# Zeroing the embedding rows of item 0: by products on TensorE, or by a multiplication on ScalarE

## The chip, the cores and the metric

One core of a Trainium2 chip runs the whole kernel. The metric is the device time of one launch in microseconds. Three runs of the kernel before took 1643.39 us in the median (1637.56 to 1649.35).

## What is computed

The inputs are 1024 sequences of 50 item numbers, their lengths, an embedding table of 100,001 rows of 128 numbers, and two vectors gamma and beta. Row 0 of the table counts as zero. Cut to what matters:

```python
emb = emb_table.at[0].set(0.0)
e = emb[seq]                                   # 1024 x 50 x 128
prefix = jnp.cumsum(e, axis=1)
denom = jnp.minimum(t_idx[None, :], lengths[:, None])
uF = prefix / denom[:, :, None]
mean = uF.mean(axis=0); var = uF.var(axis=0)
y = (uF - mean) * lax.rsqrt(var + BN_EPS) * gamma + beta
# for each of 50 time steps, x = y[:, t]:
v = v + (x - v) / 2.0
spike = (v - 1.0 >= 0)
v = v - spike
# and at the end:
scores = spikes.mean(axis=0) @ emb.T           # 1024 x 100001
```

So there is a recurrent part of 50 steps, whose result is a count of spikes per sequence and feature, and a large product with the whole table, whose output is 409.6 MB.

## The kernel before, in words

**Recurrent stage.** The 1024 sequences lie as 8 blocks (n) of 128. For each time step t the function `gather` (line 204) issues eight indirect DMAs from GpSimd (POOL), each fetching 128 table rows into one block of the tile `e`; `e` has two buffers, so the gather of step t+2 writes where step t lay. TensorE transposes each block with the identity and adds it up in PSUM (line 327): the accumulators `pre[0]` and `pre[1]` hold the running sums with features on the partitions and 512 sequences each. This document calls the eight transposes of a step T0 to T7. VectorE divides (`uF`, line 338) and takes the statistics (lines 339 and 345). ScalarE takes the root (349) and subtracts the mean (356); VectorE works out the factor `a` in a few short instructions (362 to 375); ScalarE forms x in the PSUM tile of v (379); VectorE adds the spikes of the step before to `count` (300) and finishes v (382); ScalarE copies v less 1 into `d` (293), from which VectorE forms `negv` in the next step (297).

**Item 0.** The gather fetches the real row 0 where an item is 0, and the running sums have to lose it. `zT` holds, for each step and sequence, whether the item is 0 (lines 215 to 226). `correct(t, l)` (line 279) adds, for each half of the sequences, one product of `ls` with `zT`, which subtracts row 0 where it was gathered. `only(t)` (line 266) makes the left sides `ls` for five steps at a time on VectorE. The first such product also opens the accumulation group of `pre` (start=True). `correct(t + 1, l)` is issued after the eight transposes of step t.

**The order.** The tile framework runs with a manual schedule: each engine takes its instructions in the order in which the program issues them and waits by semaphores for what it needs from other engines. What stands behind a waiting instruction on its engine waits too.

**The end of the stage.** In the last step T4, T5 and T6 are each followed by four transposes that only keep TensorE busy (`keep_busy`, line 307), and T7 by sixteen more (line 414). At steps 42 and 44 the kernel also prepares the first two blocks of the table (`prepare`, line 148: eight transposes, a copy on ScalarE, a subtraction on VectorE), and after the second it fetches two more table blocks from SP (line 404). The last step is cut into pieces, so that the first output block can start when the first 128 sequences have their counts.

**Product stage.** The table comes in blocks of 1024 rows, is transposed (line 136) and split into a high and a low part (152, 153), and is multiplied with the counts of 128 sequences at a time (160). ScalarE and VectorE take turns in moving the results out of PSUM (513 and 511), and SP stores them.

**Buffers.** The pool `once` holds what lasts for the recurrent stage; after the stage its place is taken by output tiles. Its tiles `near`, `centred` and `vA` of the last step lie in the places of `r0`, `r0hi` and `r0n`.

Of the kernel before, what the change touches and what calls it, by code (L numbers as in the profile page):

```python
# [12 lines left out]
F32 = mybir.dt.float32  # L13
BF16 = mybir.dt.bfloat16
F32R = mybir.dt.float32r
I32 = mybir.dt.int32
U32 = mybir.dt.uint32
AF = mybir.ActivationFunctionType
ALU = mybir.AluOpType

P = 128
# [4 lines left out]
BANK = 512  # L26
GROUP = 6
AHEAD = 6
ONLY = 5
TWICE = 2  # L30
ASIDE = 2
SHIFT = TWICE + ASIDE
# [7 lines left out]
def rec_kernel(  # L40
# [9 lines left out]
    nc = tc.nc  # L50
    B, T = seq.shape
    N, D = table.shape
# [119 lines left out]
    with ExitStack() as ph:  # L172
# [9 lines left out]
        nc.sync.dma_start(out=idx, in_=seq.rearrange("(p n) t -> p n t", n=NB))  # L182
        len_i = once.tile([P, NB], I32, tag="len_i", name="len_i")
        nc.sync.dma_start(out=len_i, in_=lengths.rearrange("(p n) -> p n", n=NB))
        r0 = once.tile([P, D], F32, tag="r0", name="r0")
        nc.sync.dma_start(out=r0, in_=table[0:1, :].to_broadcast([P, D]))
        gb = once.tile([P, 2], F32, tag="gb", name="gb")
        nc.sync.dma_start(out=gb[:, 0:1], in_=gamma.rearrange("(d o) -> d o", o=1))
        nc.sync.dma_start(out=gb[:, 1:2], in_=beta.rearrange("(d o) -> d o", o=1))
# [22 lines left out]
                )  # L212

        make_identity(nc, ident)
        isz = up.tile([P, NB, P], F32, tag="uF", name="isz")
        rb = up.tile([P, NB, P], F32, tag="uF", name="rb")
        gather(0)

        nc.vector.memset(isz, 0.0)
        for u in (0, P // 2):  # L220
            nc.vector.tensor_single_scalar(isz[:, :, u : u + T], idx, 0.0, ALU.is_equal)
        zps = vp.tile([P, B], F32, tag="v1", name="zps")
        for n in range(NB):
            nc.tensor.transpose(zps[:, n * P : (n + 1) * P], isz[:, n, :], ident)
        zT = once.tile([P, B], F32R, tag="zT", name="zT")
        nc.scalar.copy(zT, zps)
        r0hi = once.tile([P, D], F32R, tag="r0hi", name="r0hi")
        nc.scalar.copy(r0hi, r0)
        r0n = once.tile([P, D], F32, tag="r0n", name="r0n")
        nc.vector.tensor_scalar_mul(r0n, r0hi.bitcast(F32), -1.0)  # L230
        up2 = slice(P // 2, P)
        nc.vector.tensor_tensor(r0n[up2, :], r0hi[up2, :].bitcast(F32), r0[up2, :], ALU.subtract)
        sel = once.tile([P, P // 2], F32, tag="sel", name="sel")
        nc.vector.tensor_tensor(sel, ident[:, : P // 2], ident[:, P // 2 :], ALU.add)


        rl = once.tile([P, NB], F32, tag="rl", name="rl")
        nc.vector.tensor_copy(rl, len_i)
# [22 lines left out]

        pre = [accp.tile([P, BANK], F32, tag=f"pre{h}", name=f"pre{h}") for h in range(B // BANK)]

        ls = once.tile([P, ONLY, D], F32R, tag="ls", name="ls")

        def only(t):

            k = t % ONLY
            if k == 0:
                n = min(ONLY, T - t)  # L270
                nc.vector.tensor_tensor(
                    ls[:, :n, :],
                    r0n.unsqueeze(1).to_broadcast([P, n, D]),
                    sel[:, t : t + n].unsqueeze(2).to_broadcast([P, n, D]),
                    ALU.mult,
                )
            return ls[:, k, :]

        def correct(t, l):
            for h in range(B // BANK):  # L280
                nc.tensor.matmul(  # L281
                    pre[h],
                    lhsT=l,
                    rhs=zT[:, h * BANK : (h + 1) * BANK],
                    start=t == 0,
                    stop=False,
                    skip_group_check=True,
                )

        def over(t, v):  # L290

            d = lp.tile([P, B], BF16, tag="d", name=f"d_{t}")
            nc.scalar.activation(d, v, AF.Identity, bias=less)  # L293
            return d
# [4 lines left out]
        def spiked(out, cs, v):  # L299
            nc.vector.scalar_tensor_tensor(out, v, V_TH, count[:, cs], ALU.is_ge, ALU.add)  # L300
# [9 lines left out]

        v = None

        correct(0, only(0))
        l = only(1)
        gather(1)
        for t in range(T):
            last = t == T - 1
            e = es.pop(t)
            if last:
                rest(d, v, pieceA)  # L320
                near = once.tile([P, P], F32, tag="r0", name="near")
                nc.vector.tensor_scalar(near, negv[:, :P], -0.5, hgb[:, 1:2], ALU.mult, ALU.add)
            uF = up.tile([P, B], F32, tag="uF", name=f"uF_{t}")
            bs = sp.tile([P, B // BANK, 6], F32, tag="bs", name=f"bs_{t}")
            for h, cs in enumerate(halves):
                for k in range(0, BANK, P):
                    nc.tensor.matmul(  # L327
                        pre[h][:, k : k + P],
                        lhsT=e[:, h * BANK + k : h * BANK + k + P],
                        rhs=ident,  # L330
                        start=False,
                        stop=last,
                        is_transpose=True,
                        skip_group_check=True,
                    )
                    if last and h and k + P < BANK:
                        keep_busy(ident, KQ // 2)
                nc.vector.scalar_tensor_tensor(uF[:, cs], rlen[:, cs], 1.0 / (t + 1), pre[h], ALU.max, ALU.mult)  # L338
                nc.vector.bn_stats(bs[:, h, :], uF[:, cs])  # L339
            if t + 2 < T:  # L340
                gather(t + 2)
            if not last:
                correct(t + 1, l)
            mv = sp.tile([P, 2], F32, tag="mv", name=f"mv_{t}")
            nc.vector.bn_aggr(mv, bs.rearrange("p h s -> p (h s)"))  # L345


            r = sp.tile([P, 1], F32, tag="r", name=f"r_{t}")
            nc.scalar.activation(r, mv[:, 1:2], AF.Sqrt, bias=eps)  # L349
            if last:  # L350
                centred = once.tile([P, P], F32, tag="r0hi", name="centred")
                nc.vector.tensor_scalar(centred, uF[:, :P], mv[:, 0:1], hgb[:, 2:3], ALU.subtract, ALU.mult)
                w = sp.tile([P, 1], F32, tag="w", name="w")
                nc.vector.tensor_scalar_add(w, mv[:, 1:2], BN_EPS)
            else:
                nc.scalar.activation(uF, uF, AF.Identity, bias=mv[:, 0:1], scale=-1.0)


            if t and not last:
                rest(d, v, whole)  # L360

            nc.vector.reciprocal(r, r)
            q = sp.tile([P, 1], F32, tag="q", name=f"q_{t}")
            a = sp.tile([P, 1], F32, tag="a", name=f"a_{t}")
            if last:
                nc.vector.tensor_scalar(q, w, r, r, ALU.mult, ALU.mult)
                nc.vector.scalar_tensor_tensor(q, q, 3.0, r, ALU.subtract, ALU.mult)
                vA = once.tile([P, P], F32, tag="r0n", name="vA")
                nc.vector.scalar_tensor_tensor(vA, centred, q, near, ALU.mult, ALU.add)
                spiked(countA, slice(0, P), vA)  # L370
                nc.vector.tensor_mul(a, q, hgb[:, 0:1])
            else:
                nc.vector.scalar_tensor_tensor(q, mv[:, 1:2], BN_EPS, r, ALU.add, ALU.mult)
                nc.vector.tensor_scalar(q, q, r, 3.0, ALU.mult, ALU.subtract)
                nc.vector.tensor_scalar(a, q, r, hgb[:, 0:1], ALU.mult, ALU.mult)  # L375


            def x(vt, cs):
                nc.scalar.activation(vt, uF[:, cs], AF.Identity, bias=hgb[:, 1:2], scale=a)  # L379

            def step(vt, cs):
                nc.vector.scalar_tensor_tensor(vt, negv[:, cs], -0.5, vt, ALU.mult, ALU.add)  # L382

            if not last:
                vt = vp.tile([P, B], F32, tag=f"v{t % 2}", name=f"v_{t}")
                x(vt, whole)
                if t:
                    spiked(count, whole, v)
                step(vt, whole)
                v = vt  # L390
                if t == T - 2:
                    spiked(count, whole, v)
                d = over(t, v)
                if t + 2 < T:
                    l = only(t + 2)

                if t in (T - 8, T - 6):
                    q = (t - T + 8) // 2
                    pair(q)
                    prepare(q, vp.tile([P, HALF], F32, tag="v1", name=f"pt_{q}"))  # L400
                    if q == TWICE - 1:
                        for k in range(TWICE):
                            rows[GROUP + ASIDE + k] = first[:, k, :]
                        nc.sync.dma_start(
                            out=first[:, :TWICE, :],
                            in_=table[(GROUP + ASIDE) * HALF : (GROUP + SHIFT) * HALF, :].rearrange(
                                "(q p k) d -> p q (k d)", p=P, k=KQ
                            ),
                        )

        keep_busy(near, 2 * KQ)
# [138 lines left out]
```

## Time and profile before

| | |
|---|---|
| median of three runs | 1643.39 us |
| the profiled execution | 1576.4 us |
| its span in the trace | 1574.6 us |
| first and last gather on POOL start | 3.6 and 504.5 us |
| POOL busy | 380.9 us in 406 instructions |
| ScalarE (ACT) busy | 673.4 us |
| VectorE (DVE) busy | 949.3 us |
| TensorE (PE) busy | 1128.4 us |
| written to memory | 409.60 MB |

In the profile, a line such as "L207" is a line of the kernel below. A row of the groups gives the line, the engine, the operation, the tiles written and read, the count, then the busy time in microseconds and the mean of one in nanoseconds, then the idle time ahead of these instructions and what ended it. "PEld" is the load of the stationary operand. "issue" is time in which an engine waited for nothing that the profile shows. A line of the timeline gives the start and the duration in microseconds, and in brackets the idle time before it with what ended it. The chain of waits is followed back from the last instruction, at each step to what released it.

### The profile page before, as it was taken

What the parts mean: (1) busy time and instruction counts of PE and PEld (TensorE: products, weight loads), DVE (VectorE), ACT (ScalarE), POOL (GpSimd) and SP (SyncE); (2) the same over time, 40 slices, a digit from 0 to 9 for tenths busy, and PEclk for the clock granted to TensorE, in tenths of its full rate; (3) what the DMA queues carried; (4) which work ended last, traced back from release to release, by engine and by line L of the source; (5) the groups of instructions that cost most, each with busy time, mean ns of one, the idle gap of its engine ahead of it and who ended that gap; (6) DMA issues with size and microseconds to landing.
All of it is one profiled execution on the core that took longest, in us unless ns stands there. A gap on an engine that the chain in (4) does not pass through costs nothing.

```text
span 1574.6 us, 12255 instructions
## 1 busy us (share of the span) xinstructions
PE 1128.4 (72%) x4464; PEld 799.5 (51%) x4464; DVE 949.3 (60%) x1127; ACT 673.4 (43%) x697; POOL 380.9 (24%) x406
## 2 busy tenths in 40 slices
PE   4544444444445998899888878888878878888884
PEld 2211111111122766677766666666666666666663
DVE  5777777777777655666555555555555545555552
ACT  2333333333333545555444444444444444444442
POOL 7777777777776000000000000000000000000000
PEclk9999999999975999999999999898999999999998
DMA  9711111111121899999999999999999999999998
GB/s 347 264 52 54 52 54 52 53 53 54 52 79 47 337 414 414 423 413 402 428 427 429 427 426 421 421 409 429 421 428 424 402 428 429 414 423 417 426 405 354
DMA packets 51313, 488.12 MB, mean 310 GB/s; under 512 B 10079, under 2 KB 10336, under 8 KB 30004
## 3 DMA queue, kind: packets, MB, share of 16 engines
q1 hardware_dynamic: 30752, 430.86, 65.1%
q0 software_dynamic: 12800, 26.24, 5.7%
q10 hardware_dynamic: 7700, 30.23, 4.7%
q8 instruction: 35, 0.57, 0.1%
q14 instruction: 26, 0.21, 0.0%
HBM read 77.69 MB, written 409.60 MB: 309 GB/s over the span
## 4 chain that ended last, share of the span: by engine, by line
DMA 48%; POOL 18%; PE 15%; issue 8%; DVE 5%; ACT 4%; ACTq 0%; SPq 0%; POOLq 0%; DVEq 0%
DMA scores<-o 42%; POOL e L207 18%; PE po L160 14%; DMA e<-in_L_rec_emb_table,idx 6%; DVE o L511 3%; ACT o L513 3%; DVE pairs L153 1%; ACT pairs L152 0%; PE pt L136 0%; ACT hi L152 0%; DVE lo L153 0%; PE pre L327 0%; DMA idx<-in_r_seq 0%; DVE bs L339 0%; DVE uF L338 0%
## 5 line engine op out<-in xcount | busy, mean ns | idle before, releaser
L511 DVE TENSOR_SCALAR o<-po 128x1024 f32<-128x1024 f32 (+1 forms) x391 | 467.3, 1214 | 329.5 <-DMA scores<-o 187.4
L513 ACT ACTIVATE o<-po 128x1024 f32<-128x1024 f32 x391 | 392.0, 1025 | 506.0 <-DMA scores<-o 362.7
L207 POOL DMA_INDIRECT e<-in_L_rec_emb_table,idx x400 | 380.2, 951 | 123.9 <-issue 112.5
L327 PE MATMUL pre<-ident,e 128*128 128x128 f32 x400 | 179.9, 463 | 227.3 <-DMA e<-in_L_rec_emb_table,idx 227.0
L160 PE MATMUL po<-pairs,countB 128*128 128x512 f32 (+1 forms) x1120 | 292.8, 408 | 57.8 <-ACT o L513 57.8
L160 PE MATMUL po<-pairs,countC 128*128 128x512 f32 (+1 forms) x840 | 240.1, 433 | 59.4 <-ACT o L513 53.4
L160 PEld LDWEIGHTS po<-pairs,countB 128*128 128x128 f32 x1120 | 211.8, 194 | 119.2 <-ACT o L513 76.7
L327 PEld LDWEIGHTS pre<-ident,e 128*128 128x128 f32 x400 | 73.4, 184 | 337.1 <-DMA e<-in_L_rec_emb_table,idx 336.4
L160 PEld LDWEIGHTS po<-pairs,countC 128*128 128x128 f32 x840 | 168.1, 208 | 112.1 <-ACT o L513 65.5
L153 DVE TENSOR_TENSOR pairs<-pt,pairs 128x1024 fp32r<-128x1024 f32 x70 | 85.2, 1218 | 94.9 <-ACT pairs L152 94.8
L338 DVE SCALAR_TENSOR_TENSOR uF<-rlen,pre 128x512 f32<-128x512 f32 x100 | 68.3, 683 | 109.6 <-PE pre L327 109.6
L136 PE MATMUL pt<-ident,rows 128*128 128x128 f32 (+1 forms) x768 | 104.4, 281 | 9.9 <-issue 4.9
L349 ACT ACTIVATE r<-mv,eps 128x1 f32<-128x1 f32 x50 | 14.7, 295 | 223.4 <-DVE mv L345 223.4
L136 PEld LDWEIGHTS pt<-ident,rows 128*128 128x128 f32 (+1 forms) x768 | 94.1, 147 | 27.1 <-issue 10.9
L160 PE MATMUL po<-hi,countB 128*128 128x512 f32 x208 | 85.6, 411 | 15.1 <-ACT o L513 13.5
L281 PE MATMUL pre<-zT,ls 128*128 128x512 f32 x100 | 77.5, 777 | 23.2 <-DVE uF L338 19.3
L152 ACT CAST pairs<-pt 128x1024 fp32r<-128x1024 f32 x70 | 70.1, 1014 | 41.2 <-PE pt L136 41.2
L160 PE MATMUL po<-lo,countB 128*128 128x512 f32 x208 | 83.4, 401 | 0.0
L293 ACT ACTIVATE d<-v,less 128x1024 bf16<-128x1024 f32 x49 | 54.6, 1114 | 64.8 <-DVE v L382 62.3
L160 PE MATMUL po<-hi,countC 128*128 128x512 f32 x156 | 66.7, 427 | 14.1 <-ACT o L513 12.6
L379 ACT ACTIVATE v<-uF,hgb,a 128x1024 f32<-128x1024 f32 x49 | 59.2, 1208 | 30.6 <-DVE a L375 30.5
L339 DVE BATCH_NORM_STATS2 bs<-uF 128x6 f32<-128x512 f32 x100 | 69.4, 694 | 3.5
(87 smaller groups left out, 851.8 us busy)
## 6 DMA issues: line engine op xcount, KB each, us to landing
scores<-o SPq DMA_DIRECT2D x96, 3072.0 KB, 19.8
scores<-o SPq DMA_DIRECT2D x32, 1536.0 KB, 8.9
scores<-o SPq DMA_DIRECT2D x30, 1024.0 KB, 7.9
rows<-in_L_rec_emb_table ACTq DMA_DIRECT2D x19, 1536.0 KB, 29.3
scores<-o SPq DMA_DIRECT2D x8, 2896.5 KB, 17.2
rows<-in_L_rec_emb_table SPq DMA_DIRECT2D x5, 3072.0 KB, 34.9
e<-in_L_rec_emb_table,idx POOLq DMA_INDIRECT x400, 2.5
rows<-in_L_rec_emb_table SPq DMA_DIRECT2D x2, 1024.0 KB
```

What stands on the lines that cost most here:

```text
L136: nc.tensor.transpose(pt[:, k0 : k0 + pw], r[:pw, k0 : k0 + D], ident[:pw, :pw])
L152: nc.scalar.copy(vh, vp)
L153: nc.vector.tensor_tensor(vl, vp, vh.bitcast(F32), ALU.subtract)
L160: nc.tensor.matmul(po[:, :kw], lhsT=counts[n], rhs=part[:, k0 : k0 + kw], start=j == 0, stop=j == 1,)
L207: nc.gpsimd.indirect_dma_start(out=es[t][:, n * P : (n + 1) * P], out_offset=None, in_=table, in_offset=bass.IndirectOffsetOnAxis(ap=idx[: ...
L281: nc.tensor.matmul(pre[h], lhsT=l, rhs=zT[:, h * BANK : (h + 1) * BANK], start=t == 0, stop=False, skip_group_check=True,)
L327: nc.tensor.matmul(pre[h][:, k : k + P], lhsT=e[:, h * BANK + k : h * BANK + k + P], rhs=ident, start=False, stop=last, is_transpose=True, ...
L338: nc.vector.scalar_tensor_tensor(uF[:, cs], rlen[:, cs], 1.0 / (t + 1), pre[h], ALU.max, ALU.mult)
L339: nc.vector.bn_stats(bs[:, h, :], uF[:, cs])
L379: nc.scalar.activation(vt, uF[:, cs], AF.Identity, bias=hgb[:, 1:2], scale=a)
L511: nc.vector.tensor_scalar_mul(o[:, h0 : h0 + hw], po[:, :hw], 1.0 / T)
L513: nc.scalar.mul(o[:, h0 : h0 + hw], po[:, :hw], 1.0 / T)
```

## The change

Where an item is 0, the gathered row is now multiplied by 0, and by 1 elsewhere. `some` holds these factors. For each block of each step ScalarE runs one in-place multiplication of 128 by 128 elements with one factor per partition (sequence), `masked`. For step t+1 these are issued within step t: blocks 0 to 3 between x (379) and the copy `d` (293), blocks 4 to 7 after `d` (and, at steps 42 and 44, after the copy of the table block). The eight of step 0 come before the loop. The products `correct`, their left sides `only`, and the tiles for them are gone. The accumulation groups are opened by one product per half with `count`, which is zero at that time.

```diff
-        r0 = once.tile([P, D], F32, tag="r0", name="r0")
-        nc.sync.dma_start(out=r0, in_=table[0:1, :].to_broadcast([P, D]))
...
-        nc.vector.memset(isz, 0.0)
-        for u in (0, P // 2):
-            nc.vector.tensor_single_scalar(isz[:, :, u : u + T], idx, 0.0, ALU.is_equal)
...
+        some = once.tile([P, NB, T], F32, tag="some", name="some")
+        nc.vector.tensor_single_scalar(some, idx, 0.0, ALU.is_gt)
...
-        def only(t):
...
-        def correct(t, l):
...
+        def masked(t, ns):
+
+            for n in ns:
+                part = es[t][:, n * P : (n + 1) * P]
+                nc.scalar.activation(part, part, AF.Identity, scale=some[:, n, t : t + 1])
...
-        correct(0, only(0))
-        l = only(1)
+        for h in range(B // BANK):
+            nc.tensor.matmul(
+                pre[h],
+                lhsT=count[:, :P],
+                rhs=count[:, h * BANK : (h + 1) * BANK],
+                start=True,
+                stop=False,
+                skip_group_check=True,
+            )
+        masked(0, range(NB))
         gather(1)
...
             if t + 2 < T:
                 gather(t + 2)
-            if not last:
-                correct(t + 1, l)
...
                 if t == T - 2:
                     spiked(count, whole, v)
+                masked(t + 1, range(NB // 2))
                 d = over(t, v)
-                if t + 2 < T:
-                    l = only(t + 2)
-
                 if t in (T - 8, T - 6):
...
+                masked(t + 1, range(NB // 2, NB))
```

More of the change, by code (lines that the diff above doesn't have):

```diff
@@ L28 @@
 AHEAD = 6
-ONLY = 5
 TWICE = 2
@@ L214, in rec_kernel @@
         make_identity(nc, ident)
-        isz = up.tile([P, NB, P], F32, tag="uF", name="isz")
         rb = up.tile([P, NB, P], F32, tag="uF", name="rb")
         gather(0)
-        nc.vector.memset(isz, 0.0)
-        for u in (0, P // 2):
-            nc.vector.tensor_single_scalar(isz[:, :, u : u + T], idx, 0.0, ALU.is_equal)
[L222 to L234, printed above, removed]
+        some = once.tile([P, NB, T], F32, tag="some", name="some")
+        nc.vector.tensor_single_scalar(some, idx, 0.0, ALU.is_gt)
         rl = once.tile([P, NB], F32, tag="rl", name="rl")
@@ L262, in rec_kernel @@
         pre = [accp.tile([P, BANK], F32, tag=f"pre{h}", name=f"pre{h}") for h in range(B // BANK)]
-        ls = once.tile([P, ONLY, D], F32R, tag="ls", name="ls")
-        def only(t):
[L268 to L277, printed above, removed]
-        def correct(t, l):
[L280 to L288, printed above, removed]
+        def masked(t, ns):
+            for n in ns:
+                part = es[t][:, n * P : (n + 1) * P]
+                nc.scalar.activation(part, part, AF.Identity, scale=some[:, n, t : t + 1])
         def over(t, v):
```

## The prediction

> **What bounds the kernel now.** I read the table of stretches first, then the chain of waits over two parts, then the groups, then one step of the loop in the timeline.
>
> ```profile
> 300.00:400.00 100.00, 47.54 (x100) 19.00 (x100) 71.91 (x123) 36.62 (x41) 75.62 (x81) 1.00 0.18 53
> 1000.00:1574.00 574.00, 460.11 (x1992) 361.12 (x1990) 297.36 (x252) 248.05 (x250) 0.00 (x0) 0.92 0.98 416
> ```
>
> Busy us of PE, PEld, DVE, ACT and POOL, then clock, DMA share and GB/s. There are two stages. Up to about 510 us the cell runs 50 time steps: POOL is busiest (75.6 of 100), the DMA engines carry 18%. After it the product writes 409.6 MB with the DMA engines at 98%. The change touches the first stage only, so it counts by how much later the first product starts. The chain of waits over 150 to 260 us, and two groups:
>
> ```profile
> by line: POOL e L207 57.7%; issue 23.2%; DMA e<-in_L_rec_emb_table,idx 19.5%; PE pre L327 0.4%; POOLq L207 0.1%
> ...
> L207 POOL DMA_INDIRECT e<-in_L_rec_emb_table,idx x400 | 380.2, 951 | 123.9 <-issue 112.5 <-DMA e<-in_L_rec_emb_table,idx 7.3 <-DMA idx<-in_r_seq 2.3
> L281 PE MATMUL pre<-zT,ls 128*128 128x512 f32 x100 | 77.5, 777 | 23.2 <-DVE uF L338 19.3 <-DVE ls L271 3.9
> ```
>
> POOL issues a gather of 128 rows every 0.95 + 0.30 = 1.25 us: 8 a step, 10.0 us a step, 500 us for 50. The gathers run from 3.6 to 505.4 us. The products that go (L281) are not in the chain at all. One step of the timeline shows how much room the other engines have:
>
> ```profile
> 315.45 0.94 POOL L207 DMA_INDIRECT e<-in_L_rec_emb_table,idx  x1 [0.30 <-issue]
> ...
> 316.75 0.48 PE L327 MATMUL pre<-ident,e 128*128 128x128 f32 x1 [0.77 <-DMA e<-in_L_rec_emb_table,idx]
> ...
> 318.96 0.30 ACT L349 ACTIVATE r<-mv,eps 128x1 f32<-128x1 f32 x1 [4.41 <-DVE mv L345]
> 319.16 1.13 ACT L356 ACTIVATE uF<-uF,mv 128x1024 f32<-128x1024 f32 x1
> ...
> 320.56 0.27 DVE L375 TENSOR_SCALAR a<-q,r,hgb 128x1 f32<-128x1 f32 x1
> ...
> 320.93 1.21 ACT L379 ACTIVATE v<-uF,hgb,a 128x1024 f32<-128x1024 f32 x1 [0.64 <-DVE a L375]
> 322.18 1.23 DVE L382 SCALAR_TENSOR_TENSOR v<-negv,v 128x1024 f32<-128x1024 f32 x1 [0.21 <-ACT v L379]
> 323.44 1.11 ACT L293 ACTIVATE d<-v,less 128x1024 bf16<-128x1024 f32 x1 [1.30 <-DVE v L382]
> ```
>
> Count from S = 316.75, the start of the eighth transpose T7, when its block lands. x ends at S+5.4, v is ready at S+6.66, d runs S+6.7 to S+7.8. Then ScalarE waits 4.4 us for the next step. The buffer that T7 frees is written again by a gather about 8.2 us later (307.23 to 315.45, one step earlier): POOL does not wait until the compute is 8 us late.
>
> **What the skill says.** The Trainium skill, ScalarE: Activation LUTs, What ACT_TABLE_LOAD costs: 186 ns + 0.833 ns per element, about 93 ns more for each operand that is a [128,1] pointer, and 93 ns of overlap between neighbours. The trace agrees: L349 (one pointer) takes 295 ns, yet L356 starts 0.20 us after it, and the one small copy (L228, 128x128) took 0.30 against 0.29 by the formula. SBUF — State Buffer, SBUF: two separate sides: only VectorE and GpSimd share a port, ScalarE has its own. So the masks should not stretch the gathers; before, POOL holds its 1.25 us beside ScalarE's work.
>
> **The change, part by part.**
>
> *Removed.* Setup (isz, zps, zT, r0hi, r0n, sel: DVE 0.9 + 0.65 + 0.75, ACT 1.3), 10 ls products of 0.81 us, 100 products of 0.78 us. All lie beside POOL's issue, which starts when idx lands (3.57 us) and does not wait for them: gain 0. Without the r0 load SP sends the table loads 0.46 us earlier, behind idx all the same: 0.
>
> *Added at the start.* One int compare on DVE (at most the 0.65 us of the two on L221), two products with the zero count, eight masks of step 0. Block 7 of step 0 lands at about 18.1 us, the mask ends by 18.6, and a Sqrt table load (1.28, as at 7.39 before) can fall before the 20.5 at which mv is ready. POOL first needs the freed buffer at 25.15: 0.
>
> *The masks, 392 more.* 128x128, scale by pointer. Whether the default bias is an immediate or a pointer the trace does not show: an estimate by the skill's formula is 107 + 186 + 93 = 386 ns with one pointer, 480 with two; with the overlap a pitch p of 0.29 or 0.39 us. I take 0.39 and keep 0.29 and 0.48 (no overlap). With ScalarE in order, from S:
> - x ends S+5.4; four masks from S+5.3 end at S+6.95 (blocks 0 to 3 landed by S+5);
> - d waits behind them: S+6.85 to S+7.95, against S+6.7 before;
> - four more masks: S+7.85 to S+9.5; the next T7 can start at S+9.55.
> So the loop through ScalarE needs 9.55 us (9.0 at p 0.29), and the gathers 10.0. The gathers still win by 0.45 us a step. In the steady state T7 is one mask (0.48) later than the landing; x and the gather of two steps on have 8.2 us of room for it. Stage length: no change.
>
> *POOL's waits.* A gather now overwrites a block that ScalarE wrote and PE read: perhaps one more wait per step. Such a wait shows as an event of 17 ns, 48 times before, and the gap of the gathers that have it is 0.30 like the others: 0. If all 384 had one unhidden: 6.5 us.
>
> *The end.* Here nothing covers. At step 44 the 1 MB fetch (L404) lets T7 of step 45 start at 469.37, 2.7 us late. Before, the loop (under 8 us) makes that good in one step; now it recovers 0.45 a step, so at step 48 1.35 are left. T7 of step 48 starts at 497.04 + 0.48 + 1.35 = 498.87. At this step d waits for count too, S+7.96 = 506.83 (504.98 before), ends 507.94, and the last four masks end at about 509.5. So T4 comes at 508.4, not 503.29:
>
> ```profile
> 503.29 0.48 PE L327 MATMUL pre<-ident,e 128*128 128x128 f32 x1 [0.75 <-DMA e<-in_L_rec_emb_table,idx]
> 503.56 1.06 PE L309 MATMUL warm<-ident 128*128 128x128 f32 x4
> 504.49 0.48 PE L327 MATMUL pre<-ident,e 128*128 128x128 f32 x1
> ```
>
> Each of T4 to T6 is followed by four warm-up transposes, about 0.95 us a group; they filled the 1.25 us between landings, and now stand between transposes that wait only for masks. T7 starts at 508.4 + 2.9 = 511.3 (507.01 before) and the second uF at 511.8 instead of 507.97: +3.9 us. At p 0.29 the lag is gone by step 48, T4 comes at 506.8, and the shift is +2.3. The products follow unchanged. The scratch pool is 5.3 KB smaller, so first output tiles lie on other old tiles: 0 to 2 us, taken as 0.
>
> **Sum.** 0 + 0 + 0 + 3.9: 1576.4 becomes about 1580.4 for the profiled execution. The runs shown have a median of 1643.39, 67 us above it, and no view tells where these lie; I put the same difference on it: 1647.
>
> **Rivals.**
> - *ScalarE becomes the bound* (slower). The loop takes about 6.45 + 8p; it passes 10.0 at p = 0.444. With a lost overlap (p 0.48) it is 10.38: 49 steps x 0.38 = 18.6, two table blocks prepared in the loop that are no longer made good (about 3), the tail 2.5: +24, so 1667. At p 0.55 it is +45. For: the margin is 5%, and each mask has its own wait and works in place. Against: neighbours with waits on other engines overlap in the product stage (L513 ends at 560.74, L152 starts at 560.63).
> - *POOL pays for the wait on ScalarE*: +6.5 with the tail, +10, 1654. Against: the hidden 17 ns.
> - *Lighter TensorE, faster last stage*: if the 67 us are a lower clock in the product (PE is busy 80% there at a clock of 0.92), 78 us less work before it could give back 20 of them: 1623. Against: in the profiled run the DMA engines bound that stage.
>
> **How the numbers follow.** Gathers stay the bound 0.54; POOL's wait 0.06; ScalarE the bound 0.34, well above what the price says, since the margin is thin; faster last stage 0.06. One per cent (16 us) is about what a measurement of this kernel can tell from no change. The first two lie within it: 0.60. Slower 0.34, faster 0.06. Range: no cost less the spread of the runs (6 us), 1636, up to p of about 0.51 (10.5 us a step, +30), 1674; it leaves out the faster case and the upper part of the ScalarE case.
>
> **What would show it.** Right: gathers still 1.25 us apart and in the chain of waits, with POOL's idle time "issue"; masks of 0.39 to 0.48 us at a pitch under 0.44; ScalarE idle before the mask of block 7, waiting for DMA; T7 of the last step 2 to 4.5 us later. Wrong: gathers that wait for PE or ACT from mid-stage on, masks that lead the chain, a POOL gap over 0.30, or a product stage of another length.

## The result and the profile after

The changed kernel took 1648.02 us in the median of 14 runs (1646.84 to 1649.35), the kernel before beside it 1640.7 us (14 runs, 1637.56 to 1649.35): a ratio of 1.0036, with a 95% interval of 1.0024 to 1.0048 (the ratio is taken over all runs; the two medians lie 7.3 us apart). That is some 6 us slower. It is under the one per cent that the prediction called the limit of such a measurement, but the interval is far narrower than that, so the loss is real.

One thing has to be known ahead of all numbers: the runs fell on several chips, and what they show is of two kinds. On one chip (called Q here; the profile of before in the first part looks the same) the kernel before takes 1575 us. On three others the same kernel takes 1638 to 1643 us, and so it does in the timed runs of the result; these, and the profile after, are called S. Each of these four chips was used at one time only, so a cause that goes with the hour and not with the chip is not excluded. A ratio is always one of runs taken together on one chip.

Line numbers are those of each run's own kernel. In the changed kernel L204 is the gather, L249 a multiplication (called a mask from here on), L254 the copy `d`, L296 the transposes and L307 `uF`; without the warm-ups or the masks the later ones move up by two.

The profiled execution of the changed kernel took 1647.17 us with a span of 1645.4. Its stretches in the recurrent and in the product stage (busy us and count of PE, PEld, DVE, ACT and POOL, then clock, DMA share, GB/s):

```profile
300.00:400.00 100.00, 25.15 (x74) 13.45 (x74) 64.72 (x109) 54.67 (x111) 67.88 (x72) 1.00 0.16 47
1060.00:1645.00 585.00, 467.19 (x2032) 366.64 (x2030) 303.58 (x257) 253.14 (x255) 0.00 (x0) 0.93 0.98 416
```

By these shares the product stage is what it was (98%, 416 GB/s). In the recurrent stage TensorE has halved and ScalarE risen by half, as the change says; but POOL, which should have stayed at 75.6 as the bound, is down to 67.9: 72 gathers in 100 us where there were 81. The groups show what it waits for:

```profile
L204 POOL DMA_INDIRECT e<-in_L_rec_emb_table,idx x400 | 378.7, 947 | 187.5 <-issue 107.7 <-remote 65.2 <-DMA e<-in_L_rec_emb_table,idx 7.0
...
L249 ACT ACTIVATE e<-e,some 128x128 f32<-128x128 f32 x400 | 127.3, 388 | 6.3 <-DMA e<-in_L_rec_emb_table,idx 6.1
...
L307 DVE SCALAR_TENSOR_TENSOR uF<-rlen,pre 128x512 f32<-128x512 f32 x100 | 68.7, 687 | 186.4 <-remote 95.9 <-PE pre L296 70.3 <-issue 20.2
```

The gathers themselves take 0.947 us as before, and 65.2 us of idle time are new; "remote" is a signal whose sender the trace does not show. `uF` waits 95.9 us for the same unknown. The 400 masks take 388 ns each and wait for next to nothing. This is neither of the first two rivals: ScalarE is no bound, and a gather that doesn't stop follows the one before it by 0.30 us as ever. The next experiment shows that most of these 65 us are not the change's.

### The profile page after: what moved, and what is told of

Same layout as the page of the kernel before. It is cut to its first block, busy times and chain, and to the rows that moved or that the text cites. A ratio compares the mean times of both kernels' runs of the same rounds, so it can differ in the third digit from the quotient of the medians.

```text
span 1645.4 us, 12553 instructions
## 1 busy us (share of the span) xinstructions
PE 1034.7 (63%) x4358; PEld 778.3 (47%) x4358; DVE 945.4 (57%) x1112; ACT 791.6 (48%) x1095; POOL 379.4 (23%) x406
## 4 chain that ended last, share of the span: by engine, by line
DMA 42%; DVE 17%; PE 17%; ACT 10%; issue 7%; another core or an unknown queue 6%; POOL 0%; ACTq 0%; SPq 0%; DVEq 0%
DMA scores<-o 41%; PE po L159 13%; PE pre L296 3%; DVE bs L308 3%; DVE o L476 3%; DVE uF L307 3%; ACT o L478 3%; DVE negv L258 2%; ACT e L249 2%; ACT d L254 2%; DVE v L349 2%; ACT v L346 1%; ACT uF L323 1%; DVE pairs L152 1%
## 5 line engine op out<-in xcount | busy, mean ns | idle before, releaser
L204 POOL DMA_INDIRECT e<-in_L_rec_emb_table,idx x400 | 378.7, 947 | 187.5 <-issue 107.7
L296 PE MATMUL pre<-ident,e 128*128 128x128 f32 x400 | 138.4, 474 | 412.0 <-ACT e L249 208.2
L296 PEld LDWEIGHTS pre<-ident,e 128*128 128x128 f32 x400 | 73.3, 183 | 477.0 <-ACT e L249 224.1
L159 PE MATMUL po<-pairs,countC 128*128 128x512 f32 (+1 forms) x840 | 239.0, 431 | 56.5 <-ACT o L478 49.0
L307 DVE SCALAR_TENSOR_TENSOR uF<-rlen,pre 128x512 f32<-128x512 f32 x100 | 68.7, 687 | 186.4 <-remote 95.9
L249 ACT ACTIVATE e<-e,some 128x128 f32<-128x128 f32 x400 | 127.3, 388 | 6.3 <-DMA e<-in_L_rec_emb_table,idx 6.1
L135 PE MATMUL pt<-ident,rows 128*128 128x128 f32 (+1 forms) x768 | 105.2, 282 | 18.1 <-issue 11.5
L159 PE MATMUL po<-pairs,countA 128*128 128x512 f32 x280 | 68.6, 394 | 4.0 <-ACT o L478 3.4
```

The costliest lines, as they stand in the source:

```text
L135: nc.tensor.transpose(pt[:, k0 : k0 + pw], r[:pw, k0 : k0 + D], ident[:pw, :pw])
L159: nc.tensor.matmul(po[:, :kw], lhsT=counts[n], rhs=part[:, k0 : k0 + kw], start=j == 0, stop=j == 1,)
L204: nc.gpsimd.indirect_dma_start(out=es[t][:, n * P : (n + 1) * P], out_offset=None, in_=table, in_offset=bass.IndirectOffsetOnAxis(ap=idx[: ...
L249: nc.scalar.activation(part, part, AF.Identity, scale=some[:, n, t : t + 1])
L296: nc.tensor.matmul(pre[h][:, k : k + P], lhsT=e[:, h * BANK + k : h * BANK + k + P], rhs=ident, start=False, stop=last, is_transpose=True, ...
```

## Experiments

**The kernel before again, and the changed kernel again.** Both kernels unchanged, on other chips.

Edit: none. Kernel before on chip Q: 

> The kernel before, unchanged. The profiled execution of before took 1576.4 us, the median of its runs 1640.7: 64 us are not explained. Theory 'one odd execution': this profile shows about 1640 us, with gathers that wait in mid-stage, and its steps take about 11.2 us instead of 10.0. Theory 'profiled executions are short': it shows about 1576 again. The ratio is 1.000 within 0.2% in either case.

Kernel before on a chip S: 

> The kernel before a third time, to have its profile on the chip on which the changed kernel is profiled. Theory 'the chip': where the changed kernel has gaps in its gathers this one has them too, with 1640 us; otherwise 1575 us. Ratio 1.000.

Changed kernel on the same chip S: 

> The changed kernel, unchanged. Its profiled execution on record took 1647 us and its gathers stood still for 64 us in 23 places; three relatives of it ran without any such gap in 1571 to 1573 us beside 1575.1 for before. Theory 'the standing still belongs to the changed kernel': it is there again, about 1640 to 1650 us, 1.0036 or more. Theory 'it belongs to the chip or the day and strikes before alike': no gaps where before takes 1575; then the tail of my prediction at a pitch of 0.29 us (+2.3) and 2.4 us less of gathers that VectorE holds up (the ls products gone) leave 1575, 0.999 to 1.001.

Measured on Q: 1574.96 us, ratio 1.0000 (0.9992 to 1.0009). On S: 1638.51 us, 0.9997 (0.9986 to 1.0008), and for the changed kernel 1644.18 us, 1.0034 (1.0020 to 1.0047). The gather's group of the kernel before, first on Q, then on S:

```profile
L207 POOL DMA_INDIRECT e<-in_L_rec_emb_table,idx x400 | 380.0, 950 | 123.9 <-issue 117.9 <-DMA idx<-in_r_seq 2.3 <-PE pre L327 2.1
```

```profile
L207 POOL DMA_INDIRECT e<-in_L_rec_emb_table,idx x400 | 381.1, 953 | 179.2 <-issue 112.2 <-remote 54.7 <-PE pre L281 5.5
```

The reader sees the 54.7 us of "remote" in a kernel with no mask in it. So the 67 us between the profiled execution of before and its median, which the prediction could not place, lie ahead of the product stage: from the first store to the end it is 1060 to 1061 us on both (513.08 to 1573.3 on Q, 582.84 to 1643.8 on S). The last gather starts 56.5 us later on S (560.65 against 504.19), because gathers stand still; another 13.3 us lie between it and the first store.

What stands still there is seen in the timeline of the changed kernel on S, here some rows of ScalarE, TensorE, VectorE and POOL:

```profile
220.58 1.27 ACT L249 ACTIVATE e<-e,some 128x128 f32<-128x128 f32 x4
...
221.02 1.35 PE L296 MATMUL pre<-ident,e 128*128 128x128 f32 x4 [1.02 <-ACT e L249]
...
227.18 0.69 DVE L307 SCALAR_TENSOR_TENSOR uF<-rlen,pre 128x512 f32<-128x512 f32 x1 [5.73 <-remote]
...
227.42 0.95 POOL L204 DMA_INDIRECT e<-in_L_rec_emb_table,idx  x1 [2.10 <-remote]
```

T4 to T7 are recorded as done at 222.37. Both that need them, `uF` and the gather into the freed buffer, start 4.8 and 5.05 us later, within 0.24 us of each other. On Q `uF` starts 0.04 us after T7 (below). The rows had landed, since the masks of these blocks ended at 221.85; so what is late is TensorE or its signal. Which of the two, the trace doesn't tell, for the ends of TensorE's instructions in it are modelled. Late transfers are not seen either: the packets of a gather end 1.2 to 1.3 us after its issue in the median on Q and on S alike, and never over 5.2 us. The traces of S have also lost many records of signals (7214 are kept for the kernel before, 13224 on Q), so "remote" there says only that the sender is not on record. In what follows, "a late signal" stands for such a gap of 4 to 5 us.

**Masks away, third buffer, warm-ups away (chip Q).**

```diff
 def masked(t, ns):
-    for n in ns: ...
+    return
...
-tc.tile_pool(name="gather", bufs=2)
+tc.tile_pool(name="gather", bufs=3)
...
-if last and h and k + P < BANK:
-    keep_busy(ident, KQ // 2)
```

Without multiplications: 

> The changed kernel without any of its 400 multiplications (a sequence with an item 0 then keeps row 0 in its sums; nothing else is left out). It has neither the products nor the masks. Theory 'the masks delay the step through ScalarE': faster than the changed kernel by about 7 us or more, so level with before or faster (0.990 to 1.000). Theory 'the loss comes from what was removed, the products behind T7': as slow as the changed kernel or slower, 1.0036 or more.

With three gather buffers: 

> The changed kernel with three buffers for the gathered blocks instead of two; the 4 KB come from what the change freed. POOL may then run a further 10 us ahead. Theory 'POOL stands still because late transposes hold both buffers': these waits go and the step falls from 11.2 to near 10.0 us, some 40 to 60 us less, 0.965 to 0.975 of before. Theory 'the loop through ScalarE and TensorE sets the pace itself': no change, 1.0036.

Without the warm-ups between T4 and T7 of the last step: 

> The changed kernel without the twelve warm-up transposes between T4 and T7 of the last step. My tail step says that they cost 2.9 us of the path there: 2 to 3 us faster than the changed kernel, about 1.002 of before. Theory 'the tail is no part of the loss': no difference, 1.0036, or slower if TensorE is then colder.

The changed kernel itself was not timed on this chip; the one with three buffers stands in for it. Measured, with before at 1575.09 us: no masks 1571.44 us, 0.9976 (0.9967 to 0.9986); three buffers 1573.44 us, 0.9990 (0.9983 to 0.9996); no warm-ups 1571.37 us, 0.9978 (0.9970 to 0.9987). One step of the kernel without warm-ups on Q:

```profile
309.34 1.21 ACT L344 ACTIVATE v<-uF,hgb,a 128x1024 f32<-128x1024 f32 x1 [0.64 <-DVE a L340]
...
310.48 1.26 ACT L249 ACTIVATE e<-e,some 128x128 f32<-128x128 f32 x4
310.58 1.23 DVE L347 SCALAR_TENSOR_TENSOR v<-negv,v 128x1024 f32<-128x1024 f32 x1 [0.20 <-ACT v L344]
...
311.84 1.11 ACT L254 ACTIVATE d<-v,less 128x1024 bf16<-128x1024 f32 x1
...
314.67 0.94 POOL L204 DMA_INDIRECT e<-in_L_rec_emb_table,idx  x1 [0.30 <-issue]
314.74 0.40 ACT L249 ACTIVATE e<-e,some 128x128 f32<-128x128 f32 x1 [0.82 <-DMA e<-in_L_rec_emb_table,idx]
...
315.19 0.47 PE L296 MATMUL pre<-ident,e 128*128 128x128 f32 x1 [0.74 <-ACT e L249]
315.70 0.69 DVE L305 SCALAR_TENSOR_TENSOR uF<-rlen,pre 128x512 f32<-128x512 f32 x1 [1.98 <-PE pre L296]
```

Four masks take 1.26 us: 0.39 for the first, 0.29 more for each further one. d starts 0.03 us after v is finished (310.58 + 1.23), so the masks ahead of it delay nothing. ScalarE then waits 0.82 us for block 7: the gathers, still 0.30 us apart, set the pace. The Trainium skill, ScalarE: Activation LUTs, What ACT_TABLE_LOAD costs, gives this with one pointer operand: the prediction's estimate from it was 386 ns, less 93 ns of overlap with a neighbour. The trace agrees, with 388 to 390 ns and a pitch of 0.29 us.

The warm-ups, in the timelines of the last step: first the kernel with three buffers, which has them, then the one without. The lines ahead of the last are the transposes T4 and T7, or the row of four from T4 to T7; the last is the first store.

```profile
504.33 0.47 PE L296 MATMUL pre<-ident,e 128*128 128x128 f32 x1 [2.28 <-ACT e L249]
...
507.58 0.42 PE L296 MATMUL pre<-ident,e 128*128 128x128 f32 x1
...
513.42 0.84 SPq L168 DMA_DIRECT2D scores<-o  x2
```

```profile
504.32 1.35 PE L296 MATMUL pre<-ident,e 128*128 128x128 f32 x4 [2.28 <-ACT e L249]
...
511.38 2.04 SPq L168 DMA_DIRECT2D scores<-o  x4
```

With warm-ups T4 to T7 take 3.7 us, without them 1.35; the first store moves by 2.04 us and the whole kernel by 2.07 (1573.44 to 1571.37). The two kernels differ in the third buffer too, but up to T4 they run alike (504.33 and 504.32). Counted from the start of the last gather (504.19 before, 501.92 in both others), the second `uF` of the last step comes after 3.5 us in the kernel before, 6.1 with masks and warm-ups, and 3.9 with masks alone. So the tail costs 2.6 us, 2.2 of them by the warm-ups; the prediction's tail step gives 2.3 at a pitch of 0.29. The kernel without masks keeps its warm-ups and is as fast as the one without warm-ups: on Q it is the two together that cost.

Where does the rest come from, that makes all three faster than before? In the kernel before (on Q), the gathers read at the start and near the end:

```profile
13.71 0.91 DVE L259 MEMSET negv<- 128x1024 f32 x1 [0.16 <-issue]
13.79 2.32 POOL L207 DMA_INDIRECT e<-in_L_rec_emb_table,idx  x1 [0.30 <-issue]
14.53 0.76 DVE L271 TENSOR_TENSOR ls<-r0n,sel 128x640 fp32r<-128x640 f32 x1
...
454.81 0.82 DVE L271 TENSOR_TENSOR ls<-r0n,sel 128x640 fp32r<-128x640 f32 x1
454.88 1.57 POOL L207 DMA_INDIRECT e<-in_L_rec_emb_table,idx  x1 [0.30 <-issue]
```

and without the products (the kernel without masks):

```profile
13.81 0.95 POOL L204 DMA_INDIRECT e<-in_L_rec_emb_table,idx  x1 [0.31 <-issue]
```

The gather at 13.79 took 2.32 us and ended 0.82 us after the `ls` product (L271). Two more of the kernel before are long: that at 56.35 (1.23 us, 0.81 us after the end of the L271 that starts at 55.95) and that at 454.88 (1.57). Together 1.38 + 0.29 + 0.63 = 2.3 us, in the kernel's one chain that never waits; the last gather starts at 504.2 before and at 501.9 in all three, where no gather but the first takes over 1 us. The Trainium skill, SBUF — State Buffer, SBUF: two separate sides, says that a VectorE operation with two inputs in SBUF and a GpSimd one that reads SBUF exclude each other on a shared port. The trace agrees with it in part: every long gather after the first (1.16 us, at 3.58) overlaps L271, and in the three profiles of the kernel before each of the nine long ones past the start ends 0.81 or 0.82 us after it. But the other seven products here stretch nothing: each starts 0.32 to 0.48 us after a gather did, and neither the gather nor the product takes longer than usual. What an `ls` product costs thus hangs on where it falls in the gathers' beat of 1.25 us. At 13.79 a memset on VectorE also runs; its share isn't separated.

The last stage has also become shorter: first store to end 1060.2 us before (513.08 to 1573.3) and 1058.2 with three buffers (513.42 to 1571.6). This holds on both kinds of chip: it is 1060.2 to 1061.3 in the three profiles of the kernel before and 1058.0 to 1058.7 in all eleven others. A stretch of 30 us soon after the first store, before and with three buffers:

```profile
530.00:560.00 30.00, 26.64 (x118) 20.55 (x119) 19.15 (x16) 15.61 (x17) 0.00 (x0) 0.94 0.94 389
```

```profile
530.00:560.00 30.00, 27.62 (x123) 22.02 (x124) 19.20 (x17) 15.56 (x16) 0.00 (x0) 0.94 0.99 410
```

The DMA engines are at their limit sooner (0.99 of the time against 0.94), at the same granted clock (0.94). That the output tiles now lie on other old tiles would explain it, but it wasn't tried by itself, so the cause stays open.

**What costs on the chips S.** The first theory was: signals come late, the loop with masks needs 9.0 us a step, and that leaves 1 us in 10 to make the lateness good, and so gathers stop more. A third buffer should help, and a kernel without masks should stop less. All four on one chip:

The changed kernel: 

> The changed kernel unchanged. If the kernel before runs at about 1638 us here, with gathers that stand still in mid-stage: ratio 1.002 to 1.005, first store 2 to 4 us later than before's in the same condition. If it runs at about 1575, with gathers 1.25 us apart throughout: the sum then is +2.3 us (warm-ups between transposes that wait for masks) and -2.4 us (no ls product holds up a gather), so 0.999 to 1.001, first store at about 513.3 us, last gather at about 501.9. A rival, that the masks cost by themselves, says 1.003 in both conditions.

Three buffers: 

> The changed kernel with three gather buffers instead of two; the same work. Where gathers stand still because the buffer of two steps before is freed late (TensorE's signals come about 4 us late, and the masks leave the loop 1 us to catch up), a third buffer gives POOL 10 us more room: few gaps are left, the last gather starts near 502 us, and the kernel takes about 1580 us where before takes 1638 (ratio 0.96 to 0.97). If the gathers stand still for a cause on the DMA or POOL side, the gaps stay and the ratio is 1.00. With before at 1575 both say 0.999.

No masks: 

> The changed kernel without any of its 400 multiplications: row 0 is left in the sums, this part of the computation is left out. With before at 1638: if the masks' longer loop (9.0 us where it is under 8 without them) is what makes the changed kernel lose 6 us more of standing gathers, this one has no more gaps than before: 0.994 to 0.999. If the gaps come from what was removed (products behind the eighth transpose), it has as many as the changed kernel: 1.001 to 1.003. With before at 1575: 0.997 to 0.998.

Three buffers and no warm-ups: 

> The changed kernel with three gather buffers and without the 12 warm-up transposes between the last transposes of the last step. With before at 1575: the warm-ups' 2 us go, 0.997 to 0.998. With before at 1638: as with three buffers alone, less 2 us: 0.96 to 0.97 if late freeing of the buffer is what stops the gathers, 1.00 if not.

Measured, with before at 1640.41 us: changed kernel 1646.78, 1.0035 (1.0027 to 1.0044); three buffers 1650.41, 1.0051 (1.0033 to 1.0069); no masks 1635.98, 0.9974 (0.9962 to 0.9987); three buffers without warm-ups 1648.95, 1.0043 (1.0030 to 1.0056). The theory fell for the buffers: the first stops only came later, at 66.4 and 82.5 us instead of 60.2, there are 22 in both kernels, and the 0.96 to 0.97 that was expected came out as 1.0051. And it fell for the mid-stage. The first and the last long stop ahead of step 43, in the changed kernel

```profile
60.16 0.94 POOL L204 DMA_INDIRECT e<-in_L_rec_emb_table,idx  x1 [6.58 <-remote]
...
466.31 0.95 POOL L204 DMA_INDIRECT e<-in_L_rec_emb_table,idx  x1 [3.71 <-remote]
```

and without masks

```profile
60.10 0.94 POOL L204 DMA_INDIRECT e<-in_L_rec_emb_table,idx  x1 [6.55 <-remote]
...
477.90 0.95 POOL L204 DMA_INDIRECT e<-in_L_rec_emb_table,idx  x1 [3.71 <-remote]
```

are 36 and 37 steps apart: 11.28 and 11.29 us a step. In the kernel before (70.67 to 453.42, 34 steps) it is 11.26. With or without masks and products, the stage goes at one pace there, 1.3 us a step slower than the gathers could. So in these traces masks cost nothing in mid-stage; what they cost, 10.8 us between the medians on this chip, must come later. The last transposes and the second `uF` of step 48, first in the changed kernel:

```profile
563.07 1.35 PE L296 MATMUL pre<-ident,e 128*128 128x128 f32 x4 [1.02 <-ACT e L249]
...
569.17 0.69 DVE L307 SCALAR_TENSOR_TENSOR uF<-rlen,pre 128x512 f32<-128x512 f32 x1 [5.67 <-remote]
```

and the second `uF` of the same step without masks:

```profile
556.72 0.67 DVE L305 SCALAR_TENSOR_TENSOR uF<-rlen,pre 128x512 f32<-128x512 f32 x1
```

The second `uF` of step 48 comes 12.4 us later with masks, and the first store 13.0 us (587.14 against 574.16). From the second `uF` of step 45 (537.4 with masks, 534.6 without) to it there are three steps: 22.1 us without masks, 7.4 a step; with masks 31.7, which is three times 9.0 and one late signal of 4.75 (T7 ends at 564.42). So of the 12.4 us 2.8 were there at step 45, 4.9 are the longer loop behind the 1 MB fetch of step 44, and 4.75 a late signal that the other trace doesn't have at this place. The other two profiles of the changed kernel have it there too (5.05 and 5.50 us of idle time ahead of the second `uF` of step 48).

**The masks' place in ScalarE's order.**

```diff
-masked(t + 1, range(NB // 2))
+masked(t + 1, range(NB))
 d = over(t, v)
...
-masked(t + 1, range(NB // 2, NB))
```

All eight ahead of d: 

> All eight multiplications ahead of the copy d, none behind it; the same work. Theory A, that the masks cost by the place where they stand in ScalarE's order (the last one ends 9.0 us after the transpose T7 of the step, because d of 1.11 us and four masks come after v): the last mask now ends at about 7.7 us, so where signals come late more of the lateness is made up: ratio to before 0.998 to 1.002 where the changed kernel has 1.0035. Theory B, that each mask costs by itself (one more hand-over between the landing, ScalarE and TensorE, 10.8 us for 400): no difference, 1.003 to 1.004. Where before takes 1575 us and the gathers never stop: A 0.998 to 0.999 (the last step's T7 comes 1 to 2 us earlier), B 1.000; a loss would mean that d, now waiting for the landing of block 7, delays the next step.

The last line of the edit alone, so that four are gone: 

> Only the four multiplications of blocks 0 to 3, ahead of d; those of blocks 4 to 7 are left out except at step 0, so row 0 stays in half of the sums: this part of the computation is left out. Theory A: these four lie in the 1.3 us in which ScalarE waits for v, so they cost nothing: the time of the kernel without any multiplication, 0.997 to 0.998 in both conditions. Theory B: half of the cost of all eight: about 1.0005 where before takes 1640.

Measured on a third chip S, with before at 1642.79 us: all ahead 1646.08 (1638.63 to 1646.74), 1.0006 (0.9993 to 1.0019); four only 1650.13, 1.0040 (1.0029 to 1.0051). Theory A has its figure in the first, but a ratio whose interval holds 1, medians that still lie 3.3 us apart and runs spread over 8 us are no proof. The second refutes it, and theory B too: half the masks, ahead of d, lose as much as all do on the other chips. Its groups:

```profile
L204 POOL DMA_INDIRECT e<-in_L_rec_emb_table,idx x400 | 378.7, 947 | 193.6 <-issue 190.7 <-DMA idx<-in_r_seq 2.2 <-DMA e<-in_L_rec_emb_table,idx 0.6
...
L307 DVE SCALAR_TENSOR_TENSOR uF<-rlen,pre 128x512 f32<-128x512 f32 x100 | 68.3, 684 | 189.0 <-remote 148.7 <-issue 30.0 <-PE pre L296 10.2
```

With 204 masks in place of 400 POOL is idle for 193.6 us, and `uF` waits 148.7 us for signals of unknown senders; in the kernel with all eight ahead of d, on the same chip, these are 187.2 and 141.1. The pace of mid-stage is 11.48 us a step here (106.72 to 474.24, 32 steps). Less work went with more waiting: the lateness isn't a fixed addition to a loop that could be shortened. No order of ScalarE's work was shown to win on these chips.

## Why the prediction was right, and where it was wrong

The time was right (1647 forecast, 1648.02 measured), and so was "within one per cent"; several terms of its sum were not. That the two times agree to 1 us is luck: the forecast was worked out from an execution on Q, and the loss was measured on S, where something else sets the pace.

- *What bounds the kernel, and the masks in the steady state.* Right on Q: masks of 0.39 us, gathers 1.25 us apart in the chain, ScalarE idle 0.82 us ahead of the mask of block 7. The pitch taken, 0.39 us, was too high; it is 0.29, the lower end that was kept. So the ScalarE rival, for which 0.34 was given, had no ground: the loop needs 9.0 us (steps 45 to 47 above), not 9.55. The rival's formula 6.45 + 8p would give 8.8 at that pitch and is too low there, because d then waits for v and no longer for the masks.
- *Removed, "gain 0".* This step failed. It asked whether POOL waits for the `ls` products, and it doesn't by semaphore; but they held up its gathers, by 2.3 us in three of them (1.4 of it with a memset running beside). The prediction cited the section on the shared port and applied it only to the masks, not to the VectorE operation that was to go. Three long gathers stood in the trace of before that it read (2.31 us at 13.79, 1.21 at 56.41 and 1.30 at 455.41).
- *The end.* The mechanism is right, its size too big: +2.6 us measured from the last gather to the second `uF`, where 3.9 was taken and 2.3 given for the pitch of 0.29.
- *First output tiles, "0 to 2, taken as 0".* The last stage measured -2.0 us, on the other side of zero; whether the places of the tiles do it is not shown.
- *POOL's waits.* 0, as said: the gathers' gap stays 0.30 us.
- *The 67 us above the profiled execution, "no view tells where these lie; I put the same difference on it".* This is the weak step. They lie in the recurrent stage, which the change touches, and not in the product stage, where a rival put them. On Q the terms add up to -1.7 (2.3 and 2.0 gained, 2.6 lost), as measured for the kernel with three buffers (1575.09 to 1573.44): a small gain where a loss was forecast. On S the changed kernel loses 6 us, by 1.0034 to 1.0036 on three occasions. So the forecast of +3.6 us met +5.9 (3.9 to 7.9) from a chip whose bound is not the one that it argued from.

What stays open: why TensorE or its signals are late on chips S, and why the pace is 11.3 to 11.5 us a step there whatever the kernel. Also open is how the 6 us over the kernel before divide. Its one profile on S, 1645.61 us, is of an unusually long run (median 1638.51), with a late signal of its own in step 48 (9.96 us of idle time ahead of the first `uF`), so it can't be set against the changed kernel's at the end. Shown is that without masks the changed kernel is 0.9974 of before there, so the masks are what makes it lose. Where they do so rests on three profiles with masks and one without, and that one is of a short run: of the 22 runs without masks 15 lie from 1634.1 to 1637.2 us and seven from 1640.0 to 1643.7. The masks may bring a late signal into step 48 in every run where otherwise it falls there in some; this is not shown.

## What to carry to other kernels

Where one engine's chain never waits, look for its own instructions that take longer than their group's mean before calling anything beside it free: removing VectorE operations that lie off the chain of waits can be worth more than the chain says (2.3 us here). When the profiled execution and the median differ by more than the effect in question, find where they differ (a second profile of the unchanged kernel did it here) before forecasting from either. Work that only fills a gap, such as warm-ups between landings, becomes cost as soon as the gap moves elsewhere.

## What was not expected of the hardware

- Chips (or the times at which they were used) differ in the same kernel by 4% (1575 against 1638 to 1643 us) at a granted clock of 1.00 from 100 to 400 us, within the stage where they differ. On the slower ones VectorE and POOL start 4 to 5 us after the recorded end of TensorE's last transposes, in groups, and the stage settles at 11.26 to 11.29 us a step in three kernels with different work (11.48 in a fourth).
- A VectorE product of 128x640 with two inputs in SBUF stretched the issue of a gather that began 0.07 us after it from 0.94 to 1.57 us, and seven such products left alone gathers that had begun 0.32 us or more before them. The longest gather, 2.32 us, began 0.74 us before its product, with a memset running.
